# Moving routed-expert and attention-tail work to other steps of a delta-rule scan

## The chip, the cores and the metric

One core of a Trainium2 chip runs the whole program in one launch. The metric is the device time of one execution in microseconds. Engines: PE (TensorE), DVE (VectorE), ACT (ScalarE), POOL (GpSimd), and SP (SyncE), which only issues transfers here.

## The reference, cut to what matters

Two layers work on x of shape (8, 512, 256). Each normalizes, runs an attention, adds it with a gate, normalizes, runs a feed-forward part, adds it with a gate. The shifts, scales and gates come from a small conditioning vector per batch.

```python
h = _layernorm(x) * (1 + ca) + sa
x = x + ga * _L0_attn_ref(h, ...)      # delta rule over 512 positions
h = _layernorm(x) * (1 + cb) + sb
x = x + gb * _L0_ffn_ref(h, ...)       # each row to its best of 8 experts
# second layer: softmax attention with a relative bias, then a soft mixture of 8 experts
...
def step(M, inp):                      # per batch and head, M is 16 x 16
    q_t, k_t, v_t, b_t = inp
    out_t = jnp.einsum('bnh,bnhd->bnd', q_t, M)
    retrieved = jnp.einsum('bnhd,bnd->bnh', M, k_t)
    delta = v_t - retrieved
    M = M + b_t[..., None, None] * jnp.einsum('bnh,bnd->bnhd', k_t, delta)
    return (M, out_t)
...
# out / rms * rms_weight @ Wo.T
...
top_idx = jnp.argmax(gate_logits, axis=-1)
for e in range(NUM_EXPERTS):
    mask = (top_idx == e)[..., None].astype(x.dtype)
    out = out + mask * (relu(x @ w1[e] + b1[e]) @ w2[e] + b2[e])
```

The change touches the first layer alone.

## The kernel before

**Tiles.** The 512 positions are four tiles of 128 steps. For the recurrence, batch and head (8 x 16) lie on the 128 partitions, and `scan` (L772) runs one tile's 128 steps on DVE, one after the other: each step multiplies the state with a key (L785), forms the rank-one term (L801), reduces (L810), and updates the state (L815) and the next delta (L819). So DVE carries a chain of some 512 steps. All else of layer 0 is meant to lie beside it.

**What runs beside a scan.** During the scan of tile i three sorts of work run. `front(i + 1)` (L494) loads x, normalizes it, projects q, k and v, scales them (the multiplications L653 on POOL), and at the end turns K and V into the scan's layout (`heads`, ACT copies L734). `follow(i - 1)` (L1481) takes the tile whose scan has just ended. `rest` is what `follow` of the scan before left over.

**What `follow` does.** First comes `attend` (L853), over eight batches b: `turn` (PE transposes L885 and L888, ACT copies L892 and L897), `scores` (sixteen PE matmuls L911 into four banks), `mask` (ACT copies L926, POOL selects L928, POOL copy `pair` L939, of which there is one buffer), `weigh` (PE L954 and L960, ACT L970 and L972), `project` (PE L981 and L985, ACT copies of y L994 and of the mean square L995). After every fourth batch ACT takes the square root (L997) and `roots(h)` on DVE the reciprocal (L1023) of the four mean squares. Then `rest(b)`: ACT scales y (L1027), POOL multiplies by the gate (L1030), adds x (L1031) and issues the store (L1032). Then `stats(b)` on DVE (L1039, L1040); after the fourth, ACT takes the deviation's root (L137). Beside that `block_product` and `state` bring the recurrent state forward: PE L1003, DVE dm L1019, POOL bdM L1020; dm has one buffer, so the next dm waits for bdM.

Then comes `route` (L1064), a generator. `begin` makes scale and offset on DVE (rsf L143, offf L145), normalizes on ACT (L1107), turns on PE (L1112), shifts and scales on ACT (L1124), computes the gate's logits on PE (L1130) and turns the rows back (L1136, ACT L1142). The next piece, `more`, adds the bias on DVE (lg L1145). This is done for two halves of four batches. Later `more` pieces find the best expert, count rows (DVE L1170) and rank them (PE L1172, L1173, L1177; the last is kept as `issued["ranked"]`). From the ranks DVE finds the slots (over L1185 and on), and POOL scatters rows to slots.

**The slots.** `experts` (L1385) is a generator as well. There are eight slots of 168 rows per tile, one per expert, and slots beyond that for experts with more rows, under a run-time condition. A call of `on` advances one stage. The first fetches weights of slots 0 and 1 (SP L1272). Then each slot j has four stages: the inner matmuls of chunks 0 to 2 with the `back` of slot j - 1 (PE L1317 and L1355, POOL store L1364); the inner matmuls of the rest with the next load; half of the outer matmuls (L1336) with the next turn (L1302); the other half. ACT has L1325, L1341, L1307 and L1363 of it. In tiles 0 and 1, slots 0 to 5 run in the scan of `follow`, from place 78 on; slots 6 and 7 are left over for the scan after it (scans 2 and 3, counted from 0). In tile 2 only slot 7 is left over, for the time after the scans.

**The order.** Every piece has a place, a number of steps. `run` sorts the pieces by place and puts each into the program when the scan has come to that step:

```python
for s, step in enumerate(steps or ()):
    while left and left[0][0] <= s:
        with tc.issue_after(step):
            left.pop(0)[1]()
```

`tc.issue_after(step)` holds the piece's DVE instructions behind the step's own, which are on DVE too. The instructions of PE, ACT, POOL and SP stand in the order of each engine's own queue and start when their data and buffers allow. `behind(n)` (L1512) advances the slots by n stages and keeps them behind `issued["ranked"]`, whichever ranked matmul was issued last.

**The places that the change touches**, all for the tiles before the last (h is the half, b the batch):

- L1060 `rest(b)`: 27 to 30 for h = 0, 45.4 to 48.4 for h = 1
- L1061 `stats(b)`: 33 to 36 and 49 to 52
- L1506 `begin`: 38.6; the first `more` stays at 45
- L1532 the slots' first fetch: 73 in `follow(1)`, 73.5 in `follow(2)`
- L1549 the leftover slots: slot 6 at 60.3 + 2.2 i + 1.5 n for its stages n = 0 to 3, slot 7 at 6.2 more; both with `behind`

`pieces` that are not named keep their places: turn 4b, scores 4b + 2, mask 4b + 5, weigh 4b + 8, project 4b + 10, block_product 3.5b + 26, state 3.5b + 32, roots(0) 27. The ranks are made at 63 in scan 2 and at 65 in scan 3.

Of the kernel before, what the change touches and what calls it, by code (L numbers as in the profile page):

```python
# [25 lines left out]
NT = S // P  # L26
# [45 lines left out]
def tile_two_layers(ctx: ExitStack, tc: tile.TileContext, t: dict, out: bass.AP):  # L72
# [62 lines left out]
    def deviation(pool, tag, mv):  # L135
        sd = pool.tile([P, mv.shape[1]], F32, tag=f"sd{tag}", name=f"sd{tag}")
        nc.scalar.activation(sd, mv[:, :, 1], AF.Sqrt, bias=ln_eps)  # L137
        return sd
# [160 lines left out]
    with ExitStack() as l0:  # L299
# [538 lines left out]
        def most(tiles):  # L838

            first, end = tiles[0], tiles[-1] + 1  # L840
            top = w0.tile([P, 1], F32, name=f"top{first}")
            counts[tiles] = w0.tile([P, 1], mybir.dt.int32, name=f"most{first}")
            nc.vector.tensor_reduce(top, beyond[:, first:end], AX.X, ALU.max)
            nc.vector.tensor_copy(counts[tiles], top)

        def rare(tiles, homes):

            slots = nc.values_load(counts[tiles][0:1, 0:1], min_val=0, max_val=NOVER)
            with tc.If(slots > 0):
                for i in tiles:  # L850
                    general(i, homes)

        def attend(i, qk, V, x1, norms):  # L853
# [168 lines left out]
            def roots(h):  # L1022
                nc.vector.reciprocal(got["ms", h], got["ms", h])  # L1023

            def rest(b):
                y = got[b]
                nc.scalar.activation(  # L1027
                    y, y, AF.Copy, scale=got["ms", b // 4][:, b % 4 : b % 4 + 1]
                )
                ve.tensor_mul(y, y, gates[0][:, b, :])  # L1030
                ve.tensor_add(x1[b], x1[b], y)  # L1031
                (nc.sync if i == NT - 1 else nc.gpsimd).dma_start(x2d[b][i], x1[b])  # L1032

            def stats(b):
                h = b // 4
                if b % 4 == 0:
                    got["mv", h] = fp.tile([P, 4, 2], F32, tag="mvf", name=f"mvf{i}_{h}")
                st = fp.tile([P, 6], F32, tag="stf", name=f"stf{i}_{b}", bufs=4)
                nc.vector.bn_stats(st, x1[b])  # L1039
                nc.vector.bn_aggr(got["mv", h][:, b % 4, :], st)  # L1040
                if b % 4 == 3:
                    norms.append((got["mv", h], deviation(fp, "f", got["mv", h])))

            pieces = [(0, deltas), (1, tokens)]
# [11 lines left out]
            for h in range(2):  # L1056
                late = 2 if i < NT - 1 else 0
                pieces.append((16 * h + 25 + late + h * late * 0.65, lambda h=h: roots(h)))
                for b in range(4 * h, 4 * h + 4):
                    pieces.append((13 * h + 25 + late + h * late * 0.7 + b, lambda b=b: rest(b)))  # L1060
                    pieces.append((12 * h + 30 + late * 3 // 2 + b, lambda b=b: stats(b)))  # L1061
            return got, pieces

        def route(i, h, norms):  # L1064
# [178 lines left out]
        def carve(homes, flats):  # L1243

            for flat, keys in flats:
                left = 0
                for key in keys:
                    size = SIZES[key]
                    made = flat[:, left : left + int(np.prod(size))]
                    if len(size) == 2:  # L1250
                        made = made.rearrange("p (a b) -> p a b", a=size[0])
                    homes[key] = made
                    left += int(np.prod(size))
            return homes
# [226 lines left out]
        def follow(i, qk, V):  # L1481


            x1, norms = [], []
            _, pieces = attend(i, qk, V, x1, norms)
            work = {}

            def begin():
                work["route"] = route(i, x1, norms)
                next(work["route"])  # L1490

            def more():
                next(work["route"])

            routed = routes[i] = {}
            slots = experts(i, routed)

            def settle():
                routed["slot"], routed["idx"], routed["scatter"] = next(work["route"])

            def on(n=1):
                for _ in range(n):
                    next(slots)

            places = {NT - 1: (51, 57, 60, 62), NT - 2: (53, 62, 65, 66.5)}.get(i, (53, 59, 63, 66))
            pieces += [(34 if i == NT - 1 else 38.6, begin), (42 if i == NT - 1 else 45, more)]  # L1506
            pieces += zip(places, (more, more, more, settle))
            apart = 0.01 if i == NT - 1 else 1.1
            pieces += [
                (places[-1] + apart * (b + 1), lambda b=b: routed["scatter"](b)) for b in range(B)  # L1510
            ]
            def behind(n):  # L1512
                with tc.issue_after(issued["ranked"]):
                    on(n)

            def over():
                homes = carve({}, [
                    (ap.tile(shape, F32, tag=tag, name=f"{tag}_rare", bufs=bufs).rearrange(
                        "p a b c -> p (a b c)" if len(shape) == 4 else "p a b -> p (a b)"
                    ), keys)  # L1520
                    for tag, shape, bufs, keys in (
                        ("qk", [P, 2, B, D], 1, ("w0", "act", "hTs", "yTs")),
                        ("dtok", [P, P, HD], 1, ("w1",)),
                        ("stk", [P, 4, P], 4, ("hslot",)),
                        ("stk", [P, 4, P], 4, ("ysb",)),
                    )
                ])
                most((i,))
                rare((i,), homes)

            late, opens, pace = {NT - 2: (7, 79, 6.4)}.get(i, (6, 78, 7.4))
            pieces.append(({NT - 1: 62.6, NT - 2: 73.5, 1: 73}.get(i, 67.5), on))  # L1532
            rest = []
            if i == NT - 1:
                pieces.append((62.7, over))
            elif i == NT - 2:
                pieces.append((90, lambda: most(EARLY)))
            for j in range(NE):
                if i == NT - 1:
                    rest += [(10 * j, lambda: on(2)), (10 * j + 3, lambda: on(2))]  # L1540
                elif j < late:
                    pieces += [
                        (opens + pace * (j + half / 2), lambda: on(2)) for half in range(2)
                    ]
                elif i == NT - 2:
                    rest.append((62.2 + 0.2 * (j - late), lambda: behind(4)))
                else:
                    rest += [
                        (60.3 + 2.2 * i + 6.2 * (j - late) + 1.5 * n, lambda: behind(1))  # L1549
                        for n in range(4)  # L1550
                    ]
            if i == NT - 1:
                rest += [(200, on), (250, on)]

            at, apart = [(1, 2.2), (21, 2.2), (108, 6), (0, 0)][i]
            return pieces, rest, [
                (at + apart * n, on) for n in range(B + DEPTH[i])
            ]
# [48 lines left out]
        parts, pieces, later = front(0, 0)  # L1607
        run(pieces)
        rest, gathers = [], []
        for i in range(NT):  # L1610
            pieces = rest
            if i > 0:
                last = i == NT - 1
                more, rest, behind = follow(i - 1, before["qk"], before["V"])
                gathers += behind
                pieces = pieces + more
                if last:
                    pieces = pieces + [(54, load1)]
            else:
                pieces = [  # L1620
                    (2, weights0),
                    (4, lambda: shift_scale(0, 1)),
                    (6, lambda: gate_rows(0, 0)),
                    (8, lambda: gate_rows(0, 1)),
                    (10, lambda: shift_scale(1, 0)),
                    (12, lambda: shift_scale(1, 1)),
                    (14, lambda: gate_rows(1, 0)),
                    (16, lambda: gate_rows(1, 1)),
# [5 lines left out]
            if i + 1 < NT:  # L1634
                parts, more, _ = front(i + 1, 47 if i > 0 else 30)
                pieces = pieces + more + (later if i == 0 else [])
            run(pieces, scan(i, before["K"], before["V"]))
        rare(EARLY, carve({}, [(w1["strips"].rearrange("p n s -> p (n s)"), tuple(SIZES))]))
        banks.append("spare")
        more, last, _ = follow(NT - 1, before["qk"], before["V"])  # L1640
        strips = [
            (1 + p0 / 3, lambda p0=p0: load_strips(p0)) for p0 in range(0, P, COPIES)
# [17 lines left out]
    with ExitStack() as l1:  # L1660
# [255 lines left out]
        for n in range(B * STEP + 4):  # L1916
            b, m = divmod(n, STEP)
# [7 lines left out]
            if m == 4:  # L1925
                if b + 1 < B:
                    more = list(prologue(b + 1, got[b + 1], xs))
# [133 lines left out]
```

## Time and profile before

| what | value |
|---|---|
| median of 3 runs | 1964.59 us (1957.53 to 1972.09) |
| profiled execution | 1960.66 us, span 1958.9 us |
| mean granted clock of PE | 0.882 |
| DVE busy over the span | 1533.3 us (78%) |
| PE busy over the span | 1553.7 us (79%) |
| ACT busy, POOL busy | 1014.8 us, 449.8 us |
| scans 0 to 3, from to (us) | 54 to 282, 282 to 510, 510 to 737, 737 to 967 |
| first layer's end and second layer | 967 to 1959 |

A scan is short of other work when DVE is busy from its start to its end. So the table by stage is read for DVE's busy time against the window's length, and the list of waits for what DVE waited for: each line names the engine, the instruction that waited with its line, the engine and line that released it, the total, how often, and the longest. A line of the timeline has the start, the duration, the engine, the line, the operation, output and inputs with shapes, the count of instructions in the group, and in brackets the idle time before it with the releaser.

### The profile page before, as it was taken

The numbers are of one execution on the slowest core, as the hardware profiler recorded it, in microseconds if no ns is written. First come the engines' busy times: TensorE is split into PE (matmuls) and PEld (weight loads), VectorE is DVE, ScalarE is ACT, GpSimd is POOL, SyncE is SP. The second block draws the span as 40 slices with busy tenths as digits, with TensorE's granted clock in tenths as the row PEclk, the third lists the DMA queues.
The fourth block names the chain that finished last, engine by engine and source line by source line (L and its number), as shares of the span: only waits on it lengthen the run. The fifth ranks groups of instructions, "written<-read, shape, count | busy, mean of one in ns | idle before, by whom it ended". The sixth has DMA issues, their size and how long they took to land.

```text
span 1958.9 us, 31975 instructions
## 1 busy us (share of the span) xinstructions
PE 1553.7 (79%) x10698; PEld 1104.0 (56%) x10698; DVE 1533.3 (78%) x5615; ACT 1014.8 (52%) x2371; POOL 449.8 (23%) x706
## 2 busy tenths in 40 slices
PE   4424137578886888759896988999999999999998
PEld 4312125448665686558775975666565656565553
DVE  4999999999989999899863017767677777777755
ACT  4325134565555655423342348886767576666630
POOL 1213014242243422520262121001010101010221
PEclk8657568589986999869996998999999999999999
DMA  8720000025202452126773852000010100000011
GB/s 265 235 79 11 0 1 12 16 92 179 94 12 65 132 186 85 41 78 222 230 148 109 244 166 58 7 20 17 17 26 20 25 15 20 20 20 9 18 25 16
DMA packets 86011, 148.73 MB, mean 76 GB/s; under 512 B 9440, under 2 KB 66720, under 8 KB 77392
## 3 DMA queue, kind: packets, MB, share of 16 engines
q1 hardware_dynamic: 67490, 117.63, 18.9%
q0 software_dynamic: 15584, 25.67, 6.5%
q10 hardware_dynamic: 2766, 3.30, 0.5%
q8 instruction: 88, 1.44, 0.3%
q14 instruction: 83, 0.68, 0.1%
HBM read 106.11 MB, written 40.47 MB: 75 GB/s over the span
## 4 chain that ended last, share of the span: by engine, by line
PE 48%; DVE 27%; issue 10%; ACT 7%; POOL 4%; DMA 3%; SPq 0%; POOLq 0%; ACTq 0%; DVEq 0%
PE ps L1872 9%; PE ps L1725 7%; DVE sums L810 5%; DVE upd L801 5%; DVE state L815 5%; DVE terms L785 5%; PE ps L1687 4%; PE ps L1748 4%; PE ps L1317 3%; PE ps L1336 3%; DVE kept L819 2%; PE ps L267 2%; PE ps L581 2%; PE ps L1801 1%; PE ps L911 1%
## 5 line engine op out<-in xcount | busy, mean ns | idle before, releaser
L1712 ACT ACTIVATE pr<-pr,low 128x256 f32<-128x256 f32 (+3 forms) x512 | 251.4, 553 | 131.4 <-DVE low L1700 131.0
L1700 DVE CUSTOM_DVE_ANT_0 pr<-ps,strips 128x256 f32<-128x256 f32 (+3 forms) x512 | 219.1, 485 | 42.6 <-PE ps L1687 41.7
L1872 PE MATMUL ps<-ew,hTd 128*128 128x512 f32 x512 | 247.5, 611 | 0.0
L810 DVE TENSOR_REDUCE sums<-terms 128x17 f32<-128x289 f32 x508 | 228.7, 450 | 0.0
L815 DVE TENSOR_TENSOR state<-state,upd 128x256 f32<-128x256 f32 x511 | 216.8, 424 | 0.0
L785 DVE TENSOR_TENSOR terms<-state,K 128x256 f32<-128x256 f32 x512 | 212.8, 416 | 0.0
L801 DVE TENSOR_TENSOR upd<-K,kept 128x256 f32<-128x256 f32 x511 | 210.9, 413 | 0.1
L1877 DVE SCALAR_TENSOR_TENSOR accd<-ps,wtd,accd 128x256 f32<-128x256 f32 x256 | 123.2, 481 | 76.1 <-PE ps L1872 65.9
L1725 PEld LDWEIGHTS ps<-cst,pr 128*128 128x128 f32 x1280 | 147.1, 144 | 50.0 <-issue 33.4
L1336 PE MATMUL ps<-act,w 128*128 128x168 f32 x1024 | 162.3, 312 | 16.0 <-ACT yTs L1341 11.6
L1725 PE MATMUL ps<-cst,pr 128*128 128x128 f32 x1280 | 164.9, 280 | 7.1 <-ACT pr L1712 5.6
L1317 PE MATMUL ps<-hTs,w 128*128 128x168 f32 x1024 | 162.7, 314 | 3.3 <-ACT hTs L1307 3.3
L1336 PEld LDWEIGHTS ps<-act,w 128*128 128x128 f32 x1024 | 149.6, 191 | 22.9 <-ACT yTs L1341 16.9
L1317 PEld LDWEIGHTS ps<-hTs,w 128*128 128x128 f32 x1024 | 153.7, 196 | 4.8 <-ACT hTs L1307 4.0
L1872 PEld LDWEIGHTS ps<-ew,hTd 128*128 128x128 f32 x512 | 89.2, 191 | 97.8 <-issue 75.8
L1325 ACT ACTIVATE act<-ps,w 128x168 f32<-128x168 f32 x256 | 85.0, 398 | 100.0 <-PE ps L1317 86.0
L1882 POOL TENSOR_TENSOR accd<-accd,bc_g 128x256 f32<-128x256 f32 x28 | 20.3, 724 | 448.4 <-DVE accd L1877 441.2
L819 DVE SCALAR_TENSOR_TENSOR kept<-kept,sums 128x16 f32<-128x16 f32 x508 | 119.3, 235 | 0.0
L1733 DVE COPY prT<-ps 128x384 f32<-128x384 f32 (+1 forms) x192 | 110.2, 592 | 5.8 <-PE ps L1725 5.2
L1687 PE MATMUL ps<-kT,qTc 32*128 32x128 f32 (+3 forms) x1024 | 106.2, 472 | 3.8 <-ACT prT L1731 2.2
L1731 ACT COPY prT<-ps 128x384 f32<-128x384 f32 (+1 forms) x192 | 92.4, 507 | 19.2 <-PE ps L1725 18.2
L926 ACT COPY stk<-ps 128x512 f32<-128x512 f32 x96 | 52.4, 622 | 74.6 <-PE ps L960 71.0
(311 smaller groups left out, 3031.3 us busy)
## 6 DMA issues: line engine op xcount, KB each, us to landing
w<-in_wrows SPq DMA_DIRECT2D x32, 1029.0 KB
w<-in_wrows SPq DMA_DIRECT2D x32, 1024.0 KB
hs<-zero SPq DMA_DIRECT2D x4, 2352.0 KB
ys<-ysb POOLq DMA_DIRECT2D x32, 168.0 KB
hslot<-hs SPq DMA_DIRECT2D x25, 168.0 KB
x<-in_x SPq DMA_DIRECT2D x32, 128.0 KB
strips<-strip_d SPq DMA_DIRECT2D x16, 256.0 KB
out<-accd POOLq DMA_DIRECT2D x32, 128.0 KB
```

The source lines that it names most:

```text
L785: nc.vector.tensor_mul(term[:, :HD, :HD], M, K[:, s, :].unsqueeze(1).to_broadcast([P, HD, HD]))
L801: nc.vector.tensor_mul(upd, K[:, s, :].unsqueeze(2).to_broadcast([P, HD, HD]), delta(s).unsqueeze(1).to_broadcast([P, HD, HD]),)
L810: nc.vector.tensor_reduce(sums, term, AX.X, ALU.add)
L815: done = nc.vector.tensor_sub(M, M, upd)
L819: done = nc.vector.scalar_tensor_tensor(delta(s + 1), keys[:, s % KEPT, :], sums[:, HD : HD + 1], sums[:, :HD], ALU.mult, ALU.subtract, re ...
L1317: nc.tensor.matmul(ph[:, q * CAP : (q + 1) * CAP], w[:, k * FF + f * P : k * FF + (f + 1) * P], hT[:, k, :], start=(k == 0), stop=(k == 1),)
L1336: nc.tensor.matmul(py[:, c * CAP : (c + 1) * CAP], w[:, f * D + c * P : f * D + (c + 1) * P], act[:, f, :], start=(f == 0), stop=(f == NFC ...
L1687: made = nc.tensor.matmul(pscs[r][:, at[i]], qT[rows, g, o, i * P : (i + 1) * P], kT[rows, g, :W], start=True, stop=True,)
L1700: nc.vector.tensor_tensor_reduce(out=pr[:, at[i]], in0=pscs[r][:, at[i]], in1=strips[:, n, S - (i + 1) * P :], scale=1.0, scalar=3.0e38, o ...
L1712: nc.scalar.activation(pr, pr, AF.Exp, bias=low, scale=-1.0)
L1725: made = nc.tensor.transpose(pt[:, n * P : (n + 1) * P], prs[r, i][:, j * P : (j + 1) * P], ident)
L1872: nc.tensor.matmul(pe, hT[0][:, k, cols], ew[:, k, e : e + 2, :], start=(k == 0), stop=(k == 1),)
```

## The change

It moves places and nothing else; no instruction is added or removed.

- The first half's rests go from 27, 28, 29, 30 to 27, 29, 31, 33; its statistics from 33 to 36 to 35.5 to 38.5. The second half stays.
- `begin` goes from 38.6 to 41.2.
- The first weight fetch goes from 73 to 67.5 in `follow(1)` and from 73.5 to 70 in `follow(2)`.
- In tiles 0 and 1 the leftover slot 6 runs at 7, 12, 17 and 22 of the next scan, with a plain `on`; slot 7 at 63.3 + 2 i + 1.6 n, behind the ranks.

From the edit on, lines stand six further down (L1145 becomes L1151).

```diff
                 for b in range(4 * h, 4 * h + 4):
-                    pieces.append((13 * h + 25 + late + h * late * 0.7 + b, lambda b=b: rest(b)))
-                    pieces.append((12 * h + 30 + late * 3 // 2 + b, lambda b=b: stats(b)))
+                    pieces.append((
+                        25 + 13 * h + b if i == NT - 1 else (27 + 2 * b, 41.4 + b)[h],
+                        lambda b=b: rest(b),
+                    ))
+                    pieces.append((
+                        30 + 12 * h + b if i == NT - 1 else (35.5, 45)[h] + b,
+                        lambda b=b: stats(b),
+                    ))
...
-            pieces += [(34 if i == NT - 1 else 38.6, begin), (42 if i == NT - 1 else 45, more)]
+            pieces += [(34 if i == NT - 1 else 41.2, begin), (42 if i == NT - 1 else 45, more)]
...
-            pieces.append(({NT - 1: 62.6, NT - 2: 73.5, 1: 73}.get(i, 67.5), on))
+            pieces.append(({NT - 1: 62.6, NT - 2: 70}.get(i, 67.5), on))
...
-                    rest += [
-                        (60.3 + 2.2 * i + 6.2 * (j - late) + 1.5 * n, lambda: behind(1))
-                        for n in range(4)
+                    rest += [(7 + 5 * n, on) for n in range(4)] if j == late else [
+                        (63.3 + 2 * i + 1.6 * n, lambda: behind(1)) for n in range(4)
                     ]
```

## The prediction

> **What bounds the kernel now.** I read the table by stage first, then the list of VectorE's waits, then the timelines around each wait. One execution: 1960.66 us, of which 1958.9 are the span. The three timed runs have the median 1964.59; with the profiled one, four executions have the median 1962.6, so the profiled one lies 1.9 below. The sum is made on it and moved up by 1.9.
>
> In the table by stage (columns: window and its length, then busy time and count of PE, PEld, DVE, ACT, POOL, then clock, DMA share, GB/s) the four scans lie at 54 to 282, 510, 737 and 967 us:
>
> ```profile
> 282.00:510.00 228.00, 167.21 (x1144) 134.68 (x1136) 227.04 (x896) 127.41 (x323) 75.25 (x131) 0.82 0.25 85
> 510.00:737.00 227.00, 184.45 (x1268) 151.37 (x1269) 213.18 (x836) 126.89 (x332) 81.56 (x141) 0.87 0.27 88
> 737.00:967.00 230.00, 181.29 (x1359) 159.06 (x1357) 220.00 (x865) 93.77 (x253) 58.39 (x92) 0.87 0.39 131
> ```
>
> VectorE (DVE) is busy for nearly all of each: it is the bound, and only its idle time, 13.8 us in scan 2 and 10.0 in scan 3, can be won. After 967 us nothing is edited. The list of waits says what the idle time is (us in total, times, longest):
>
> ```profile
> DVE stf L1039 <- POOL x L1031: 8.2, 4, 3.7
> DVE over L1185 <- PE ps L1177: 4.5, 2, 3.4
> DVE terms L781 <- ACT V L734: 4.1, 1, 4.1
> DVE rsf L143 <- ACT sdf L137: 4.0, 2, 2.0
> ...
> DVE dm L1019 <- POOL bdM L1020: 0.8, 2, 0.4
> DVE ms L1023 <- ACT ms L997: 0.5, 1, 0.5
> ```
>
> All these lie in scans 2 and 3; scan 1 has only a 0.7 wait for the counts. By scan: 2 has stf 1.37 + 1.57, dm 0.42, rsf 2.01, over 3.36, V 4.09; 3 has ms 0.46, stf 3.69 + 1.58, dm 0.42, rsf 2.01, over 1.16.
>
> **The change part by part.** Only VectorE's instructions are held by the steps; the other engines run in the order in which their instructions stand. So I read the orders of the built kernels.
>
> *Statistics later (33 to 36 becomes 35.5 to 38.5).* In the new order the first statistics stand three steps later (a step is 228 / 128 = 1.8 us), at about 565 in the working below, and the four rests then end by 564.7. The stf waits (2.94, 5.27) go. Removed, with rsf (2.01 each) and the old dm waits: -5.37 in scan 2, -7.70 in scan 3. Next late are the three items below.
>
> *Logits later (begin 38.6 becomes 41.2, the add stays at 45).* In the order rsf goes from step counter 40 to 43 while lg L1145 stays at 46. Today:
>
> ```profile
> 571.71 0.18 DVE L143 RECIPROCAL rsf<-sdf 128x4 f32<-128x4 f32 x1 [2.01 <-ACT sdf L137]
> ...
> 582.29 0.16 DVE L1145 TENSOR_TENSOR lg<-ps,gbias 128x32 f32<-128x32 f32 x1
> ```
> ```profile
> 580.60 0.43 PE L1130 MATMUL ps<-gw,hTf 128*128 128x8 f32 x2
> ```
>
> The chain rsf, ACT norm, PE, ACT, PE takes 571.71 to 581.03, 9.3 us; in scans 1 and 3 (341.13 to 350.44, 813.83 to 823.16) also 9.3. DVE's six steps cover it today with 10.6. Three steps give 5.3, 5.5 with what else stands there: a new wait of 9.3 - 5.5 = 3.8 in each of scans 1, 2 and 3. The bounds are 0 (a chain of 5.5, though its ACT and PE work stands in the same order) and 4.0. All later steps of the scan queue behind it on DVE.
>
> *Slot 6 of tiles 0 and 1 among the first steps.* Its pieces leave 617 to 632 and enter attend's ring, in which weigh(b) of PE releases ACT's copies, POOL's selects, and weigh(b+1). The slot's PE work is today:
>
> ```profile
> 618.23 1.88 PE L1317 MATMUL ps<-hTs,w 128*128 128x168 f32 x12
> 619.94 0.60 PE L1355 MATMUL ps<-cst,yTs 128*84 128x128 f32 x4
> ...
> 623.02 3.01 PE L1317 MATMUL ps<-hTs,w 128*128 128x168 f32 x20
> ...
> 626.40 0.34 PE L1177 MATMUL ps<-cst,count 64*128 64x8 f32 x2
> 626.66 2.55 PE L1336 MATMUL ps<-act,w 128*128 128x168 f32 x16
> ```
>
> with the turn (0.46) and a second 2.55, 11.0 in all. In the ring PE has little room:
>
> ```profile
> 507.06 1.15 PE L911 MATMUL ps<-qT,kTa 32*128 32x256 f32 x16 [2.94 <-ACT qT L897]
> ...
> 525.74 1.98 PE L911 MATMUL ps<-qT,kTa 32*128 32x256 f32 x16
> ```
>
> In 523 to 530 PE is busy 6.60 of 7.00 us, and sixteen score matmuls that need 1.15 take 1.98, paced by the banks: room of about 0.4 + 0.8 = 1.2 to 1.4 per batch. In the new order the first twelve inner matmuls and a back turn (2.5) stand ahead of weigh(0), with 0.5 more for the slow clock there: 3.0. The twenty (3.0) stand between scores(2) and weigh(1), almost bare: 2.9. The two outer halves stand around project: 3.0 - 1.4 = 1.6 and 2.5 - 1.4 = 1.1. The ring is late by D = 8.6; the bounds are 2 (it hides in the gaps of all five batches) and 15 (11.0 of PE and 5 of ACT, less one gap). I take 8.6, since the rows place each piece.
>
> The square root for ms L1023 ends at 541.29 in scan 2, 2.4 ahead of DVE at 543.65. Through project(3) it comes 8.4 later: a new wait of 8.4 - 2.4 = 6.0. In scan 3 DVE waits already: +8.4. Behind it stand the scan's next steps on DVE, and ACT's and POOL's rests.
>
> The clock: in 503 to 515 the granted clock is 0.72 and L888 takes 0.42, from 515 it is 1.00 and 0.27. By this row the first piece is slow, which the 0.5 holds. The Trainium skill (TensorE: Matmul & The Clock Gate, section Part 1: The HAM clock gate) says that the clock opens after some 3.4 us of sustained work. By it the added matmuls would open the clock earlier for the ring, and D would be about 1 smaller, the sum 2 smaller; by the row the matmuls from 507 have holes of 2.9 and 2.1 and stay slow until 515. I keep the row.
>
> *Rests every two steps.* ACT and POOL aren't held by steps, and in the new order the four rests of the first half stand in one block on POOL, ahead of the selects of batch 6 and of bdM L1020; today selects stand among them:
>
> ```profile
> 554.20 0.72 POOL L1030 TENSOR_TENSOR y<-y,gate 128x256 f32<-128x256 f32 x1 [0.78 <-ACT y L1027]
> ...
> 557.65 0.64 POOL L928 TENSOR_SCALAR_AFFINE_SELECT stk<-stk 128x512 f32<-128x512 f32 x1
> ...
> 563.24 0.73 POOL L1020 TENSOR_TENSOR bdM<-bdM,dm 128x256 f32<-128x256 f32 x1
> ```
>
> The block takes 4 x (0.69 + 0.69 + 0.57) = 7.8 with its DMA issues. It can start at 548.3 + 8.6 = 556.9 (end of the selects of batch 5); then pair and selects 2.8, bdM 0.7: 568.2. DVE has its first dm at 552.39 + 6.0, and the second, now ahead of all statistics, 6.7 later at 565.1. New wait: 3.1 in scans 2 and 3, between 0 (block interleaved as now) and 5 (block 2 later). The ring's end is then about 6 late, before rsf's new place, so rsf doesn't wait.
>
> *Slot 6 away from the ranks, slot 7 after them.* The ranked matmuls L1172 to L1177 stand behind the twelve and the twenty today; in the new order ahead of slot 7: over falls from 3.36 to about 0.2 and from 1.16 to 0: -3.2, -1.16. At the end of scan 2 POOL's last by_head block stands behind a slot's DMA at 718.19, and so V is late by 4.09. With 11.0 us of PE work gone ahead of that slot it should come early enough: -3.5, between 0 and -4.09.
>
> *First weight fetch earlier* (73 to 67.5, 73.5 to 70): SP issues two fetches ahead of one x load; SP is on no chain there. Nothing, with the buffers' release as the cover; bounds 0 and 1.
>
> | scan | new | removed | sum |
> |---|---|---|---|
> | 1 | 3.8 | 0 | +3.8 |
> | 2 | 6.0 + 3.1 + 3.8 | 5.37 + 3.2 + 3.5 | +0.8 |
> | 3 | 8.4 + 3.1 + 3.8 | 7.70 + 1.16 | +6.5 |
>
> Together +11.1: 1960.66 becomes 1971.8, and the median of four, 1962.6, becomes 1973.7.
>
> **The rivals.** (a) *The slot fits into the ring*, D = 2: speaks for it PE's 0.40 gap and the bank pacing, against it that scores and weigh follow gapless. The ms waits are then 0 and 2, dm 2.5, lg 3.8: scan 2 -5.8, scan 3 -0.6, scan 1 +3.8, together -2.6: 1960.0. (b) *The whole slot stands in the ring's way* (the slower side), D = 15, since its ACT work, 5 us, also delays the copies: 2 x 6.4 more, +23.9: 1986.5. From D = 12.9 it is over 1% slower. (c) *No new wait at all*: every removed wait won, 5.37 + 3.2 + 3.5 + 7.70 + 1.16 = 20.9: 1941.7. Against it: the logit chain is 9.3 in all three scans. (d) *The rests' new places do nothing*, since POOL isn't held: no dm wait, 6.2 less, 1967.5.
>
> **How the numbers follow.** Chances: forecast 0.52, (a) 0.18, (b) 0.14, (c) 0.05, (d) 0.11. The prediction is 1973.7. The range 1955 to 1985 takes in (a), with the V wait's and dm's bounds below it, (d) and the lower half of (b); outside are (c) and the rest of (b), 0.12. One per cent, about what a measurement of this kernel can tell from no change, is 19.6 us. Faster by over 1% is (c) alone, 0.05; slower is most of (b), 0.11; within is 0.84.
>
> **What would show it.** New DVE waits: lg L1145 for the logits (now L1151, on PE L1136), 3 times some 3.8, the one of scan 1 too; ms L1023, some 6 and 8; dm L1019 behind bdM L1020, about 3 twice. stf, rsf and over gone, V gone from scan 2. Without an lg wait, or with ms under 3, the working is wrong; ms over 12 is (b).

## The result and the profile after

| | before | changed |
|---|---|---|
| median of 13 runs | 1966.02 us | 1975.54 us |
| profiled execution, span | 1958.9 us | 1969.0 us |
| scans, first to last state product (L785) | 53.6 to 964.3: 910.7 us | 53.9 to 975.5: 921.6 us |

The ratio of changed to before is 1.0057, 95% interval 1.0037 to 1.0076. The forecast was 1973.7 and +11.1 us; the scans alone are 10.9 us longer (11.1 from times that are not rounded to a tenth). In the change's profile the rest of the program, which it doesn't touch, takes 1969.0 - 921.6 = 1047.4 us against 1048.2.

The list of DVE's waits in the changed kernel (54 to 985 us; total, times, longest):

```profile
DVE ms L1023 <- ACT ms L997: 13.6, 2, 8.4
DVE lg L1151 <- PE ps L1136: 9.8, 3, 3.8
DVE dm L1019 <- POOL bdM L1020: 6.6, 2, 3.3
...
DVE terms L781 <- ACT V L734: 3.6, 1, 3.6
DVE count L1176 <- PE ps L1171: 1.4, 2, 0.8
```

stf, rsf and over are gone from it, 16.7 us in all; ms, lg and dm have taken their place with 30.0, where ms and dm had 1.3. V has stayed. The table by stage, cut at the first L785 of each scan, shows DVE's work unchanged and the windows longer. Before (window, length, busy of PE, PEld, DVE, ACT, POOL, clock, DMA share, GB/s):

```profile
272.00:496.80 224.80, 164.01 (x1110) 131.63 (x1110) 223.84 (x884) 127.10 (x322) 76.53 (x133) 0.82 0.21 71
496.80:736.00 239.20, 192.76 (x1336) 158.52 (x1335) 225.34 (x883) 133.87 (x345) 83.08 (x143) 0.87 0.29 98
736.00:964.30 228.30, 182.29 (x1366) 160.06 (x1364) 218.94 (x862) 94.77 (x256) 57.06 (x90) 0.87 0.38 128
```

Changed:

```profile
272.20:501.20 229.00, 164.10 (x1115) 131.79 (x1115) 224.41 (x884) 127.59 (x323) 76.54 (x133) 0.82 0.21 70
501.20:742.50 241.30, 188.89 (x1330) 156.20 (x1330) 224.83 (x883) 133.67 (x343) 83.19 (x143) 0.87 0.29 97
742.50:975.50 233.00, 179.56 (x1366) 159.14 (x1364) 218.61 (x861) 94.79 (x256) 57.12 (x90) 0.87 0.37 125
```

So scans 1, 2 and 3 grew by 4.2, 2.1 and 4.7 us, where the sum had 3.8, 0.8 and 6.5. The scans begin at 272.0, 496.8 and 736.0 us before; the bounds 282, 510 and 737 that stand ahead of the result are 1 to 13 us late. Cut at the right places, DVE's idle time before is 13.9 us in scan 2 and 9.4 in scan 3, close to the 13.8 and 10.0 that the prediction read, so the sum does not hang on it.

In the timeline of PE in scan 2 the pieces of slot 6 lie where the built order had put them:

```profile
517.14 2.73 PE L1323 MATMUL ps<-hTs,w 128*128 128x168 f32 x12
...
523.38 0.33 PE L885 MATMUL ps<-cst,qk 128*128 128x128 f32 x1
...
525.83 1.98 PE L911 MATMUL ps<-qT,kTa 32*128 32x256 f32 x16
527.74 3.12 PE L1323 MATMUL ps<-hTs,w 128*128 128x168 f32 x20
...
533.23 0.33 PE L885 MATMUL ps<-cst,qk 128*128 128x128 f32 x1
...
540.80 2.55 PE L1342 MATMUL ps<-act,w 128*128 128x168 f32 x16
...
544.81 1.15 PE L911 MATMUL ps<-qT,kTa 32*128 32x256 f32 x16
```

Before, the same turns of the following batches (L885) and the square root of the mean squares (L997):

```profile
516.50 0.33 PE L885 MATMUL ps<-cst,qk 128*128 128x128 f32 x1
...
523.29 0.33 PE L885 MATMUL ps<-cst,qk 128*128 128x128 f32 x1
...
540.99 0.30 ACT L997 ACTIVATE ms<-ms,cst 128x4 f32<-128x4 f32 x1
```

Changed:

```profile
553.01 0.30 ACT L997 ACTIVATE ms<-ms,cst 128x4 f32<-128x4 f32 x1
```

From the scan's start to the end of weigh(0) it is 22.2 us (523.38 - 501.2) against 19.7 before (516.50 - 496.8): 2.5 later. The next batch takes 9.85 in place of 6.79: 3.1. The outer halves add about 1.5 and 0.6, and the scores beside the first of them now take 1.15 in place of 1.98, which is the room that the prediction counted on. Together 7.6: the square root starts 51.8 us after the scan's start (553.01 - 501.2) against 44.2 (540.99 - 496.8). The prediction had 8.4.

### The profile page after: what moved, and what is told of

Its sections match the earlier page's. It is cut to its first block, busy times and chain, and to the rows that moved or that the text cites. A ratio compares the mean times of both kernels' runs of the same rounds, so it can differ in the third digit from the quotient of the medians.

```text
span 1969.0 us, 31973 instructions
## 1 busy us (share of the span) xinstructions
PE 1547.1 (79%) x10698; PEld 1099.3 (56%) x10698; DVE 1531.7 (78%) x5615; ACT 1015.8 (52%) x2371; POOL 450.1 (23%) x706
## 3 DMA queue, kind: packets, MB, share of 16 engines
q1 hardware_dynamic: 67490, 117.63, 18.7%
## 4 chain that ended last, share of the span: by engine, by line
PE 43%; DVE 32%; issue 9%; ACT 7%; POOL 5%; DMA 3%; SPq 0%; another core or an unknown queue 0%; POOLq 0%; ACTq 0%; DVEq 0%
PE ps L1877 9%; PE ps L1730 7%; DVE sums L810 6%; DVE state L815 6%; DVE upd L801 6%; DVE terms L785 5%; PE ps L1692 4%; PE ps L1753 4%; DVE kept L819 2%; PE ps L1342 2%; PE ps L1323 2%; PE ps L267 2%; PE ps L1806 1%; DVE terms L798 1%; PE ps L251 1%
## 5 line engine op out<-in xcount | busy, mean ns | idle before, releaser
L810 DVE TENSOR_REDUCE sums<-terms 128x17 f32<-128x289 f32 x508 | 223.8, 440 | 0.0
L815 DVE TENSOR_TENSOR state<-state,upd 128x256 f32<-128x256 f32 x511 | 211.8, 414 | 0.0
L785 DVE TENSOR_TENSOR terms<-state,K 128x256 f32<-128x256 f32 x512 | 207.7, 406 | 0.0
L801 DVE TENSOR_TENSOR upd<-K,kept 128x256 f32<-128x256 f32 x511 | 206.0, 403 | 0.1
L1323 PE MATMUL ps<-hTs,w 128*128 128x168 f32 x1024 | 167.8, 320 | 3.3 <-ACT hTs L1313 3.3
L1323 PEld LDWEIGHTS ps<-hTs,w 128*128 128x128 f32 x1024 | 157.9, 201 | 6.1 <-ACT hTs L1313 4.1
L1342 PEld LDWEIGHTS ps<-act,w 128*128 128x128 f32 x1024 | 150.5, 192 | 18.2 <-ACT yTs L1347 15.4
L819 DVE SCALAR_TENSOR_TENSOR kept<-kept,sums 128x16 f32<-128x16 f32 x508 | 114.4, 225 | 0.0
L1753 PE MATMUL ps<-prT,v 128*32 128x128 f32 (+2 forms) x1536 | 90.3, 353 | 0.3 <-DVE low L1705 0.3
```

What stands on the lines that cost most here:

```text
L785: nc.vector.tensor_mul(term[:, :HD, :HD], M, K[:, s, :].unsqueeze(1).to_broadcast([P, HD, HD]))
L801: nc.vector.tensor_mul(upd, K[:, s, :].unsqueeze(2).to_broadcast([P, HD, HD]), delta(s).unsqueeze(1).to_broadcast([P, HD, HD]),)
L810: nc.vector.tensor_reduce(sums, term, AX.X, ALU.add)
L815: done = nc.vector.tensor_sub(M, M, upd)
L1323: nc.tensor.matmul(ph[:, q * CAP : (q + 1) * CAP], w[:, k * FF + f * P : k * FF + (f + 1) * P], hT[:, k, :], start=(k == 0), stop=(k == 1),)
L1342: nc.tensor.matmul(py[:, c * CAP : (c + 1) * CAP], w[:, f * D + c * P : f * D + (c + 1) * P], act[:, f, :], start=(f == 0), stop=(f == NFC ...
```

## The experiments

One thing about the numbers first: in the twelve profiles the part outside the scans, unedited in all, takes 1047 to 1059 us. So beside the time ratio I give the scans' own length, from the first to the last L785 of the profiled execution, which is 910.7 before and 921.6 changed. The ratio rests on all fast runs of a kernel, the scans' length on one execution. Scan 0, which no kernel edits, takes 217.9 to 218.3 us in all twelve.

**The first add of the logits later.** Against the changed kernel:

```diff
-            pieces += [(34 if i == NT - 1 else 41.2, begin), (42 if i == NT - 1 else 45, more)]
+            pieces += [(34 if i == NT - 1 else 41.2, begin), (42 if i == NT - 1 else 48.5, more)]
```

> The changed kernel with the first add of the logits (lg) at 48.5 in place of 45, so that six steps, at least 10 us, stand again between rsf and lg as before the change. Theory: the chain of 9.3 us is covered, the three lg waits, 9.8 us, go, and nothing after them is late: -9.8 us, equal to the kernel before (1.000). Rival (the second half's chain or the counts take the time back): lg waits gone, but new waits at the second rsf, the second lg or the counts, and less than half of it won, ratio over 1.003.

Measured: ratio 1.0006 (0.9988 to 1.0024), as the theory said; scans 912.8 us, 8.8 less than changed. The waits of this kernel:

```profile
DVE ms L1023 <- ACT ms L997: 14.5, 2, 8.4
DVE dm L1019 <- POOL bdM L1020: 6.9, 3, 3.3
...
DVE count L1176 <- PE ps L1171: 2.0, 2, 1.3
```

No lg line is left, and little came back (ms + 0.9, counts + 0.6). The lg wait was a loss by itself, and 3.5 places cure it.

**begin back.** Against the changed kernel, `41.2, begin` becomes `38.6, begin`.

> The changed kernel with begin back at 38.6. Theory (the lg waits come from rsf standing three steps later, but in scans 2 and 3 the ring of attend with slot 6 in it sets when the deviation's root is there): the lg waits, 9.8 us in the profile, go, yet rsf must now wait for ACT's L137, which ended at 582.5 and 828.3 while DVE would come at about 579.4 and 824.1: rsf waits of some 3 and 4 us, and about 1 in scan 1. Net about -2 us against the changed kernel, 1.007 down to about 1.005 against the kernel before. Rival (the later begin is a loss by itself): no rsf wait, -9.8 us, equal to the kernel before.

Measured: ratio 1.0050 (1.0027 to 1.0073), scans 919.6 us, 2.0 less than changed, as the theory said; the rival falls. The waits:

```profile
DVE ms L1023 <- ACT ms L997: 14.1, 2, 8.2
DVE rsf L143 <- ACT sdf L137: 6.7, 2, 4.0
```

The lg line has turned into an rsf line: the root of the deviation stands on ACT behind project(7), at the end of the ring. Where a late ring lies behind it, undoing an edit moves the wait and doesn't remove it. In scan 1, without leftover slots, the rsf wait was 0.06 where the theory had about 1, and the lg wait there, 3.8, was won.

**Slot 6 back.** Against the changed kernel:

```diff
-                    rest += [(7 + 5 * n, on) for n in range(4)] if j == late else [
+                    rest += [(60.3 + 2.2 * i + 1.5 * n, lambda: behind(1)) for n in range(4)] if j == late else [
```

> The changed kernel with slot 6 of tiles 0 and 1 back at 60.3 + 2.2 i + 1.5 n, behind the ranks. Theory as the prediction had it (slot 6 alone delays the ring; the rests' new places make POOL's block, hence dm): ms waits, 13.6 us, fall to 0.5, dm stays at 6.6, over returns with 4.5: -8.6 us, ratio to before 1.001. Second theory (from the built orders: the selects stand among the rests again when slot 6 is gone, and the old stf waits only hid that bdM stands behind the rests): ms 0.5, lg about 11, over 4.5, dm waits of about 4.8 in scan 2 and 7.2 in scan 3, no stf wait: about -2 us against the changed kernel, ratio to before about 1.005.

Measured: ratio 1.0044 (1.0026 to 1.0063), scans 920.8 us. The second theory was right; the prediction's own reading of the block fell:

```profile
DVE dm L1019 <- POOL bdM L1020: 13.0, 2, 7.6
DVE lg L1151 <- PE ps L1136: 11.2, 3, 3.8
DVE over L1191 <- PE ps L1183: 5.1, 2, 3.4
...
DVE ms L1023 <- ACT ms L997: 1.0, 1, 1.0
```

ms lost 12.6 us, and dm and over took back 6.4 and 5.1, lg 1.4. On POOL the selects (L928) stand among the rests again, though the rests kept their new places:

```profile
559.80 0.73 POOL L1030 TENSOR_TENSOR y<-y,gate 128x256 f32<-128x256 f32 x1 [0.78 <-ACT y L1027]
560.61 0.73 POOL L1031 TENSOR_TENSOR x<-x,y 128x256 f32<-128x256 f32 x1
561.29 0.64 POOL L928 TENSOR_SCALAR_AFFINE_SELECT stk<-stk 128x512 f32<-128x512 f32 x1
...
569.38 0.73 POOL L1020 TENSOR_TENSOR bdM<-bdM,dm 128x256 f32<-128x256 f32 x1
```

In either order bdM comes after all rests. The kernel before waited at stf for the same rests that dm waits for here: dm waits 5.41 us in scan 2 and 7.61 in scan 3, and the stf, dm and rsf waits of the kernel before were 5.37 and 7.70 together. With the slot taken out of the ring, the scans are only 0.8 us shorter than changed.

**Rests back.** Against the changed kernel, `(27 + 2 * b, 41.4 + b)[h]` becomes `(27 + b, 41.4 + b)[h]`.

> The changed kernel with the first half's rests back at 27, 28, 29, 30. As the prediction had it (the rests' new places put POOL's four rests into one block): selects stand among the rests again and the dm waits, 3.3 twice, shrink. Second theory (slot 6 makes the block): POOL's order and the dm waits stay as they are, 6.6 us in all, and the span stays within 1 us of 1969.0.

Measured in one execution: scans 922.2 us, 0.6 more than changed. The span, 1974.3, is 5.3 more, not within 1 us: 1052 of it lie outside the scans, against 1047. And

```profile
DVE dm L1019 <- POOL bdM L1020: 6.6, 2, 3.3
```

The same to a tenth. POOL's order in the built kernel is the changed one's. So slot 6 makes the block, and the rests' new places change nothing that the trace shows. The next run, with the slot and the rests' old places, has the block too.

**Slot 6 alone.** Against the kernel before:

```diff
-                    rest += [
+                    rest += [(7 + 5 * n, on) for n in range(4)] if j == late else [
                         (60.3 + 2.2 * i + 6.2 * (j - late) + 1.5 * n, lambda: behind(1))
                         for n in range(4)
                     ]
```

> The kernel before with one part alone: slot 6 of tiles 0 and 1 at 7, 12, 17 and 22. Theory (the ring gets later by some 8.5 us, and everything of the first half that waits for the ring waits in turn): ms waits of about 6 and 8.4, POOL's rests in one block, dm waits of about 3.4 twice, rsf waits of 4 to 6 each, no stf waits, no over waits: scan 2 about +5, scan 3 about +8.5, together +13.5 us, ratio about 1.007. Rival (the slot in the ring costs only what the ms waits show, 14 us, and the over waits of 4.5 are saved; stf, dm and rsf as before): about +9.5 us, 1.005.

Measured: ratio 1.0023 (1.0005 to 1.0041), scans 915.1 us, 4.4 more than before: less than both. The kinds of the waits are as the theory had them, their sizes not:

```profile
DVE ms L1023 <- ACT ms L997: 14.2, 2, 8.2
DVE rsf L143 <- ACT sdf L137: 6.9, 3, 3.9
...
DVE dm L1019 <- POOL bdM L1020: 4.3, 2, 2.2
DVE terms L781 <- ACT V L734: 2.9, 1, 2.9
```

I had put 14.4, 8 to 12 and 6.8. My reading, which no run tests by itself, is that the statistics ahead of the second dm and one wait passing its time to the next made each later one smaller. Against before that is ms + 13.7, rsf + 2.9, dm + 3.5, less stf 8.2, over 4.5, V 1.2 and counts 0.7: + 5.5, of which the scans show 4.4.

**State later.** Against the changed kernel:

```diff
-                    pieces.append((3.5 * b + 26, lambda b=b: block_product(b)))
-                    pieces.append((3.5 * b + 32, lambda b=b: state(b)))
+                    pieces.append((3.5 * b + 32, lambda b=b: block_product(b)))
+                    pieces.append((3.5 * b + 38, lambda b=b: state(b)))
```

> The changed kernel with block_product and state six places later (3.5 b + 32 and 3.5 b + 38), so that the first dm stands behind the statistics. Theory (in scans 2 and 3 the ring's end sets the time, waits only travel): the dm waits, 6.6 us, go, but rsf then comes to DVE 3.3 + 0.7 us earlier than today and waits for ACT's L137: about 2.4 in scan 2 and 3.6 in scan 3. Net about -1 us against the changed kernel. Rival (dm's wait is a loss by itself): -6.6 us, ratio to before 1.002.

Measured: ratio 1.0026 (1.0008 to 1.0044), which holds the rival's 1.002 and not the theory's 1.005. The scans, 918.8 us, are 2.8 less than changed, nearer to the theory's 1 than to the rival's 6.6. The waits:

```profile
DVE ms L1023 <- ACT ms L997: 14.4, 2, 8.4
DVE lg L1151 <- PE ps L1136: 10.6, 3, 3.5
DVE rsf L143 <- ACT sdf L137: 4.8, 2, 3.0
```

dm is gone, and 4.8 of its 6.6 stand at rsf now, 1.8 in scan 2 and 3.0 in scan 3. That the wait travels is shown; how much of the time is won stays open between 2.8 and what the ratio allows.

**All of it later, and slot 6 out of the ring.** The changed kernel with the state places above, `43.5, begin`, the first add at 51.5, the first weight fetch back at 73 and 73.5, and

```diff
-                    rest += [(7 + 5 * n, on) for n in range(4)] if j == late else [
-                        (63.3 + 2 * i + 1.6 * n, lambda: behind(1)) for n in range(4)
-                    ]
+                    rest += [
+                        (63.3 + 2 * i + 6.2 * (j - late) + 1.5 * n, lambda: behind(1))
+                        for n in range(4)
+                    ]
```

> The rest kept out of the ring's way: rests and statistics of the changed kernel, begin at 43.5, the first lg add at 51.5, block_product and state six places later, both leftover slots of tiles 0 and 1 behind the right ranks at 63.3 + 2 i + 6.2 (j - 6) + 1.5 n, first weight fetch as before the change. Theory: the ring is as in the kernel before; stf 8.2, rsf 4.0, dm 0.8 and over 4.5 go, one stf wait of about 1.6 stays in scan 3: -15.9 us against the kernel before, ratio 0.992. Rival (the waits travel on, to lg, the counts or V): under half of it, over 0.996.

Measured: ratio 0.9915 (0.9882 to 0.9949), median 1946.84 us, scans 896.8: faster than both kernels. The table by stage for its scans 2 and 3, and its waits:

```profile
497.80:729.00 231.20, 191.07 (x1332) 158.48 (x1331) 223.94 (x883) 133.15 (x343) 83.42 (x143) 0.89 0.30 101
729.00:951.10 222.10, 184.13 (x1353) 161.61 (x1352) 218.32 (x862) 94.46 (x254) 57.30 (x90) 0.85 0.38 127
```
```profile
DVE terms L781 <- ACT V L734: 5.0, 1, 5.0
DVE ms L1023 <- ACT ms L997: 1.4, 1, 1.4
...
DVE dm L1019 <- POOL bdM L1020: 1.2, 2, 0.6
DVE rsf L143 <- ACT sdf L137: 1.0, 1, 1.0
```

DVE's busy time is within 1.4 us of before in each of these scans; the scans are 8.0 and 6.2 shorter. Of the kernel before's 24.1 us of waits about 12 are left, V's 5.0 the largest.

**The same with slot 6 in the ring**: that kernel with the changed kernel's places for slots 6 and 7.

> all_later with the slots of tiles 0 and 1 as in the changed kernel: slot 6 at 7, 12, 17 and 22, slot 7 behind the ranks. Theory (slot 6 in the ring costs what ms L1023 waits, whatever else is covered): ms waits of about 6 and 8.4 in place of one of 1.4, the other waits as in all_later: +13 us against it, scans of about 910 us against 896.8, ratio to before about 0.998. Rival (with all other waits covered the ring's delay is absorbed behind step 28): less than half of that, ratio under 0.995.

Measured: ratio 0.9980 (0.9961 to 0.9999), scans 913.2 us, 16.4 more than with both slots behind the ranks. The price stays whatever else is covered:

```profile
DVE ms L1023 <- ACT ms L997: 18.0, 2, 9.6
DVE rsf L143 <- ACT sdf L137: 7.1, 2, 4.2
```

By the ratios of the two kernels, 0.9980 and 0.9915, the price is about 12.8 us, the theory's 13. The profile, of the slowest of the twelve executions, shows more, and its scans are 2.5 us longer than before although the ratio is below 1. Two things are in it. rsf waits too, with begin at 43.5: the ring's end is late as well as its middle. And ms waits 9.58 us in scan 2, where the granted clock stayed at 0.50 until 22.2 us after the scan's start; in the six other kernels with slot 6 in the ring it did until 17.5 to 18.7 us, and ms waited 5.2 to 6.2.

**Ranks first, alone.** The kernel before with only the edit of the slots of the last diff.

> The kernel before with one part alone: both leftover slots of tiles 0 and 1 behind the right ranks, at 63.3 + 2 i + 6.2 (j - 6) + 1.5 n. Theory: the over waits, 4.5 us, go, stf, dm and rsf stay as in the kernel before, and V, which slot 0's late start sets, stays at about 4: -4.5 us, ratio 0.998. Rival (the slots, 2 to 3 steps later, push the slots of the next tile and V): the V wait grows by what over loses, 1.000.

Measured: ratio 0.9980 (0.9966 to 0.9994), scans 906.7 us, 4.0 less than before. over is gone, and the rest stands:

```profile
DVE stf L1039 <- POOL x L1031: 8.4, 4, 3.7
DVE rsf L143 <- ACT sdf L137: 4.5, 3, 2.0
...
DVE terms L781 <- ACT V L734: 3.4, 1, 3.4
```

**V.** all_later with the slots opened at 75.5 in scan 2.

> As all_later, and in scan 2 the slots open at 75.5 in place of 78, so that slot 0's first turn stands ahead of one projection of the next tile. Theory (V is late because slot 0 starts only after the projection that the step's normalization paces, not because of the leftover slots): the V wait of scan 2, 3.5 to 4.1 in all kernels so far, shrinks by 2 to 4 us, ratio about 0.990. Rival (the slots' own pace of some 10 us sets V): V wait unchanged, as all_later.

Measured: ratio 0.9907 (0.9879 to 0.9935), scans 894.9 us. The V wait of scan 2 falls from 5.05 to 1.99, but the scan doesn't get shorter: 233.2 us against 231.2, and the time can't tell the kernel from all_later. Slot 0's turn comes 153.7 us after the scan's start in both, and V's copies (ACT L734) 229.4 us after it, against 227.4 in all_later. What changed is that DVE reaches V 5.1 us later, for the most part because waits at ms (1.3), stf (0.7), rsf (1.1) and ss (1.1) now stand ahead of it in this scan. The first three are in scan 3 in all_later; in each kernel they are in the scan in which the granted clock stayed at 0.50 until some 22 us after the start, and not in the one with 18. So the run doesn't show that the place of slot 0's turn sets V.

## Why the prediction was right, and where not

- **Logits later**, 3.8 in each of three scans: 3.76, 3.35 and 2.65 us. Right in kind, and more_later shows that the wait was a loss by itself. In scan 3 the term was too large by 1.2: rsf to lg's end of waiting is 828.71 to 836.86, 8.2 us, in place of 9.3. The chain goes with the granted clock over it, 0.50, 0.66 and 0.75 in scans 1, 2 and 3; in slot6_back the clock is 0.50 there in scan 3 too, and lg waits 3.75.
- **Slot 6 in the ring**, 6.0 and 8.4 at ms: waits of 5.22 and 8.38, the latter with the 0.46 of before, so 7.9 more. Right in place, and in size to 0.8, piece by piece, as the PE timeline above shows.
- **The block on POOL**, 3.1 twice at dm: 3.31 twice. The size is right and the cause was wrong. I put it down to the rests' new places; rests_back and slot6_back show that slot 6 makes it. Rival (d) was right that the rests' new places do nothing, and wrong that dm then doesn't wait: without the block it waits longer, 13.0 in slot6_back.
- **Removed waits**: the stf, rsf and dm waits of before, 5.37 and 7.70, went, but not for the reason given. The statistics' new places win nothing by themselves: in slot6_back, which has them without the slot, the same time stands at dm, 13.0. And in only_slot6, which has the slot and the statistics' old places, the stf line is gone too, because DVE, held at ms, comes later. The sum came out because both were moved together, and that is luck.
- **Ranks ahead of slot 7**, -3.2 and -1.16: the over waits, 3.36 and 1.16, are gone, and ranks_first shows -4.0 alone.
- **V, -3.5**: the step that failed; 3.65 of 4.09 stayed. I had argued that 11.0 us less of PE work would let slot 0 start earlier. It started later. Slot 0's turn and V's copies before:

```profile
658.67 0.46 PE L1302 MATMUL ps<-cst,hslot 84*128 84x84 f32 x4
...
732.20 3.64 ACT L734 ACTIVATE V<-ps 128x512 f32<-128x512 f32 x4
```

  and changed, with what stands ahead of the turn:

```profile
659.70 1.08 ACT L151 ACTIVATE xna<-xt,offa,rsa 128x256 f32<-128x256 f32 x2
660.34 0.69 PE L154 MATMUL ps<-cst,xna 128*128 128x128 f32 x2 [6.15 <-ACT xna L151]
...
666.23 0.46 PE L1308 MATMUL ps<-cst,hslot 84*128 84x84 f32 x4
...
738.70 3.64 ACT L734 ACTIVATE V<-ps 128x512 f32<-128x512 f32 x4
```

  From the scan's start the turn comes after 165.0 us in place of 161.9, V's copies after 237.5 in place of 235.4. PE stands idle for 6.15 us ahead of it and waits for the next tile's normalization xna on ACT. Its inputs rsa and offa are ready on DVE at 651.4; ACT works without a hole from 653.30 until xna, two loads of activation tables of 1.28 us among it. So it was ACT's queue that the turn waited for there, not PE's work. What sets V's time in the end stays open, as all_later_open shows. The error of 3.1 was made good by smaller lg, ms and over terms (1.6, 1.3 and 0.2), so the sum came out closer than its parts, which is luck too.
- **The clock**: the first piece ran at half clock, as the row of before had it: 2.73 us for the twelve in place of 1.88. The row's 0.72 is a mean: the trace's clock records have 1.00 up to 508.15, 0.50 up to 514.98 and 1.00 from there, and 511.88 and 518.71 in the changed kernel. The Trainium skill (TensorE: Matmul & The Clock Gate, section Part 1: The HAM clock gate) lets the clock open after some 3.4 us of sustained work. This trace agrees: after holes of 2.94 and 2.09 us PE works without a hole from 515.12, and the clock opens 3.6 us later, at 518.71; before, the stretch begins at 511.33 and the clock opens at 514.98. The added matmuls begin at 517.14, inside that stretch, and so did not open it sooner for the ring.
- **What the sum did not have**: the clock opens at another time in scan 3 than in scan 2, 21.3 us after the scan's start against 18.2 in the kernel before; there ms waited 0.46 in scan 3 and had 2.4 to spare in scan 2. In the seven kernels with slot 6 in the ring, six scans in which it opened after 17.5 to 18.7 us have ms waits of 5.2 to 6.2, and eight in which it opened after 21.6 to 22.2 have 8.2 to 9.6. The 6.0 and 8.4 of the sum hold this difference without its cause.

## What to carry to other kernels

Before a wait is removed, ask for what it waits, and who else waits for that: here stf, dm and rsf waited one after the other for work of one ring, and an edit of one place only renamed the line; lg, whose chain was just too long for the steps left to it, was won by moving it alone. A wait on the bound engine is won by moving every consumer of the late chain far enough back, the next consumer included (all_later); making the chain itself shorter was not tried. Work that fills another engine's gaps was not free inside such a ring: with the other waits covered, the same slot cost 6 to 8 us per scan inside it, and nothing that ranks_first shows behind the ranks.

## What the runs showed that I had not expected

The unedited part outside the scans varied from 1047 to 1059 us between the twelve profiled executions, as much as the whole effect under study; scan 0, paced by DVE and unedited too, stayed within 0.5 us. The variation goes with the clock: summed from the trace's clock records, the time at 0.50 after the last L785 is 76.8 to 77.3 us in the five profiles with 1047 to 1049 us outside the scans, and 81.1 to 93.5 in the seven with 1052 to 1059. No run tests which causes which. And the order of POOL's instructions changed with the place of a piece that holds none of the rests or selects: slot 6's place turned POOL's interleaved rests and selects into a block.
